# Graph attention on one core: row-by-row fetches shared by two issuing engines and counted on six semaphores

## The chip, the core and the metric

The kernel runs on one core of a Trainium2 chip. The core has a matrix engine (TensorE, "PE"; its weight loads are listed as "PEld"), a vector engine (VectorE, "DVE"), a scalar engine (ScalarE, "ACT"), a programmable engine (GpSimd, "POOL") and an engine without arithmetic that issues transfers (SyncE, "SP"). Each engine works through its own list of instructions in order. Engines wait for each other through semaphores. SP, ACT and POOL can issue DMA transfers, and sixteen DMA engines carry them out. An engine that issues a transfer is occupied while it issues; such instructions are listed as "SPq" or "ACTq".

The metric is the time of one execution on the device in microseconds (us), lower is better. A change is called faster or slower in this text when the time moves by more than 0.2%, which is about what a measurement of this kernel can tell from no change.

## The reference

One layer of graph attention with 12,500 nodes, 128 features, 8 heads of 16 features and 212,500 edges that are sorted by destination:

```python
Q = (x @ WQ).reshape(N, H, dh); K = (x @ WK)...; V = (x @ WV)...
Eh = (edge_attr @ WE).reshape(-1, H, dh)
score = K[src] * Q[dst] / sqrt(dh) * Eh
score = exp(clip(score.sum(-1, keepdims=True), -5.0, 5.0))
wV = segment_sum(V[src] * score, dst); Z = segment_sum(score, dst)
h = x + (wV / (Z + 1e-6)).reshape(N, D)
h = batch_norm(h) * gamma + beta
out = layernorm(x + h)
```

What matters here is `K[src]` and `V[src]`: for every edge one row of 256 float32 numbers (1 KB: K and V side by side) must be fetched from a table in the chip's main memory, at an address that is known only from the data.

## The kernel before

**Tiles and groups.** The edges are cut into 1661 tiles of 128 edges. Four tiles make a window and two windows make a group, so a full group `g` has 8 tiles; there are 208 groups (0 to 207), the last with 5 tiles.

**The table stage.** First the kernel multiplies all nodes with `w_kv` and writes the table `kvd` (K and V of every node) to main memory (`table_rows`, L674). For groups 0 to 7 it does not use the table: it gathers rows of `x` instead (64 gathers by POOL) and projects them itself (`project_main`). Small steps of the edge stage are laid between the steps of the table stage by the list `steps` at L706: among them `place` on the first run of windows, `load_rel` of groups 0, 1 and 2, and `turned_onehot` of groups 0 and 1.

**The gathers.** From group 8 on, each tile of 128 rows is fetched by one indirect DMA that POOL issues (`gather`, L229 and L230). It lands in one of nine buffers called `slot`, each of which holds the 8 tiles of a group. A slot is free again once `message(g)` (L615) has read it; `load_kv` (L284) then queues the gathers of the next pending group. Gathers are issued in the order of groups.

**The row fetches.** Some tiles do not go through POOL. For a group in `by_row` the last of its 8 tiles is fetched row by row: SP issues 128 transfers of 1 KB each (`fetch_rows`, L273). In each group from 8 on, SP first loads 16 node offsets into registers (L275, a `TENSOR_LOAD` on `row_ids`) and then issues 16 row transfers with these offsets (L282). So 128 rows, one tile, take 8 groups, and the tile is used 3 groups after its last row was issued: groups 18, 26, 34, ... 202, which makes 24 tiles (3072 rows). `row_plan` (L58) works out this list. The buffer `byrow` has two copies. Rows use the same eight completion semaphores in turn as all other transfers that SP and ACT issue: each transfer waits until the transfer eight places earlier on these semaphores has landed.

**The main loop (L793 to L845)** records the steps of one group after the other; each engine's order of work follows from it. In the order in which they stand: SP loads edge features four groups ahead (`load`, L495, tile `ea`, three buffers) and the transposed positions (`load_rel`, L406, tile `rb`; for groups 16 and later `load_quad`, L393, four groups at a time in tile `rbq`); then SP issues the rows of this group. DVE multiplies K with Q times E (`products`, L597), PE sums the messages of the previous group (`gather_sum`, L636), DVE reduces and clips the scores (L603, L611), ACT takes the exponential (`clip_exp`, L612 and L613) and does short copies of neighbouring groups, the last of them being `q_mid` (L555); DVE multiplies V with the scores (`message`, L621) and compares destinations (`onehot`, L526). At some groups `place` (L375) transposes the positions of the next 64 windows and writes them to `relT` in main memory; ACT issues these writes.

**The end.** After the last group a normalization over all nodes and a layer norm produce the output (`last_stage`, L920).

Of the kernel before, what the change touches and what calls it, by code (L numbers as in the profile page):

```python
# [21 lines left out]
G = 8  # L22
U = 4
WN = 64
# [5 lines left out]
ROWS = P  # L30
FIRST_ROW = 8
ROW_LAG = 3
ROW_STREAMS = (("SP", 16),)
RQ = 4


LAST = [3, 2]
# [20 lines left out]
def row_plan(sizes):  # L58


    full = sizes.count(U) // 2
    used, plan_ = set(), []
    for _, n in ROW_STREAMS:
        groups, end = [], 0
        while True:
            end += P
            g = FIRST_ROW + -(-end // n) - 1 + ROW_LAG
            while g in used:
                g += 1
            if g >= full:  # L70
                break
            used.add(g)
            groups.append(g)
        plan_.append(groups)
    return plan_


def row_groups(sizes):
    return [2 * g for groups in row_plan(sizes) for g in groups]


@with_exitstack
def gnn_kernel(
# [32 lines left out]
    dram = ctx.enter_context(tc.tile_pool(name="dram", bufs=1, space=bass.MemoryType.DRAM))  # L116
    rows = ctx.enter_context(tc.tile_pool(name="rows", bufs=1))
# [9 lines left out]
    relT = dram.tile([T, P], BF16, name="relT")  # L127

# [32 lines left out]
    rel = rel_i.bitcast(F32)  # L161
# [28 lines left out]
    ident = consts.tile([P, P], F32, name="ident")  # L190
# [58 lines left out]

    by_row, fill = {}, {}  # L250
    row_loads = []
    cols = ids = 0
    for (_, n), groups in zip(ROW_STREAMS, row_plan(usizes)):
        tot = len(groups) * P
        for q in range(-(-tot // n)):
            at = (q % P, cols + q // P * n, min(n, tot - q * n))
            fill.setdefault(FIRST_ROW + q, []).append(at + (groups, q * n))
        for q in range(0, tot // n, P):
            row_loads.append((q, min(P, tot // n - q), cols + q // P * n, n, ids + q * n))
        if tot % n:  # L260
            q = tot // n
            row_loads.append((q, 1, cols + q // P * n, tot % n, ids + q * n))
        cols += -(-tot // (P * n)) * n
        ids += tot
        by_row.update({g: None for g in groups})
# [4 lines left out]
    def parts(g, a, b):  # L270
        return [(a, b - 1), (b - 1, b)] if g in by_row and b == G else [(a, b)]

    def fetch_rows(g):  # L273
        for p, c, n, groups, at in fill.get(g, []):
            _, offs = nc.values_load_multi_w_load_instructions(  # L275
                row_ids[p:p + 1, c:c + n], engines=(ET.SP,), min_val=0, max_val=(N - 1) * 8 * P,
                skip_runtime_bounds_check_because="node ids")
            for r, off in enumerate(offs, at):
                k = groups[r // P]
                if r % P == 0:  # L280
                    by_row[k] = late[0].tile([P, 1, 2 * P], F32, name="byrow", bufs=2)
                nc.sync.dma_start(by_row[k][r % P:r % P + 1, 0, :].bitcast(U8), kvb[ds(off, 8 * P)].unsqueeze(0))  # L282

    def load_kv():  # L284
        while free and pending and table[0]:
# [54 lines left out]
    def within(f, g):  # L340
        return f(g) if 0 <= g < NG else None
# [9 lines left out]
    def vw(a, r):  # L351
        return a[:, ustarts[r[0]]:ustarts[r[0]] + (r[1] - r[0]) * r[2]].rearrange("p (g k) -> p g k", k=r[2])
# [22 lines left out]
    def place(r):  # L375
        nc.vector.tensor_copy(vw(rel, r), vw(rel_i, r))
        nc.vector.tensor_tensor(vw(rel, r), vw(rel, r), bc(base_f, r), op=OP.subtract)
        end = ustarts[r[0]] + (r[1] - r[0]) * r[2]
        for t in range(ustarts[r[0]], end, P):
            n = min(P, end - t)  # L380
            ps = spare_ps
            nc.tensor.transpose(ps[:n], rel[:, t:t + n], ident)
            row = wp.tile([P, P], BF16, name="relrow", bufs=2)
            nc.vector.tensor_copy(row[:n], ps[:n])
            nc.scalar.dma_start(relT[t:t + n, :], row[:n])

    RB = {}

    def load_quad(q):
        t = late[0].tile([P, RQ, U * P], BF16, name="rbq", bufs=2)  # L390
        for h in (0, 1):
            at = ustarts[2 * RQ * q + h] * P
            nc.sync.dma_start(t[h * WN:(h + 1) * WN], bass.AP(  # L393
                tensor=relT.tensor, offset=relT.offset + at, ap=[[0, WN], [G * P, RQ], [1, U * P]]))
        for k in range(RQ):
            RB[RQ * q + k] = t[:, k, :]

    quads = range(-(-2 * FIRST_ROW // RQ), sizes.count(G) // RQ)

    def load_rel(g):  # L400
        if g // RQ in quads:
            return
        RB[g] = wp.tile([P, U * P], BF16, name="rb", bufs=3)
        for h in (0, 1):
            t, n = ustarts[2 * g + h], usizes[2 * g + h]
            nc.sync.dma_start(RB[g][h * WN:(h + 1) * WN, :n * P],  # L406
                              bass.AP(tensor=relT.tensor, offset=relT.offset + t * P, ap=[[0, WN], [1, n * P]]))

    mv = consts.tile([P, 2], F32, name="mv")
    ab = consts.tile([P, 2], F32, name="ab")  # L410
# [180 lines left out]
    def products(g, hs=(0, 1)):  # L591
        if 0 in hs:
            PR[g] = wp.tile([P, G, P], F32, name="p", bufs=1)
        for i in hs:
            a, b = halves(g)[i]
            for c, d in parts(g, a, b):
                nc.vector.tensor_tensor(PR[g][:, c:d, :], KV[g](c, d, 0), PW[g][i][:, c - a:d - a, :], op=OP.mult)  # L597

    def scores(g, h=None):
        a, b = (0, nt(g)) if h is None else halves(g)[h]  # L600
# [14 lines left out]
    def message(g, h=None):  # L615
        if h is not None:
            ranges = parts(g, *halves(g)[h])
        else:
            ranges = halves(g) if g < nxg and g not in SLOT else parts(g, 0, sizes[g])
        for a, b in ranges:  # L620
            nc.vector.tensor_tensor(  # L621
                MSG[g][:, a:b, :P].rearrange("p t (h d) -> p t h d", d=DH),
                KV[g](a, b, P).rearrange("p t (h d) -> p t h d", d=DH),
                exp_ps(g)[:, a:b, :, None].to_broadcast([P, b - a, H, DH]), op=OP.mult)
        if g in SLOT and h != 0:
            free.append(SLOT[g])
            load_kv()
# [546 lines left out]
```

## Time and profile before

| what | value |
|---|---|
| time, median of 3 runs | 2114.01 us (2113.06 to 2116.01) |
| time of the profiled execution | 2108.13 us |
| its span (first to last instruction) | 2106.3 us |
| POOL: gathers from the table | 1573, of 948 ns each |
| SP: row transfers | 3072 |
| PE, DVE, ACT, POOL busy | 80%, 78%, 30%, 75% of the span |
| DMA engines, mean rate | 184 GB/s |

The shares of busy time are means over the whole span. Instructions that issue a DMA from SP or ACT, and loads of registers, are not counted as busy, so a small busy share of ACT does not say how much room its list of instructions has. The chain of waits follows the work that ended last backwards from the last instruction; where an engine waits for nothing that the profile shows, the time is called "issue". A gather by POOL shows as 0.95 us of work and 0.30 us of "issue" behind it.

### The profile page before, as it was taken

What the parts mean: (1) busy time and instruction counts of PE and PEld (TensorE: products, weight loads), DVE (VectorE), ACT (ScalarE), POOL (GpSimd) and SP (SyncE); (2) the same over time, 40 slices, a digit from 0 to 9 for tenths busy, and PEclk for the clock granted to TensorE, in tenths of its full rate; (3) what the DMA queues carried; (4) which work ended last, traced back from release to release, by engine and by line L of the source; (5) the groups of instructions that cost most, each with busy time, mean ns of one, the idle gap of its engine ahead of it and who ended that gap; (6) DMA issues with size and microseconds to landing.
All of it is one profiled execution on the core that took longest, in us unless ns stands there. A gap on an engine that the chain in (4) does not pass through costs nothing.

```text
span 2106.3 us, 37679 instructions
## 1 busy us (share of the span) xinstructions
PE 1692.8 (80%) x9414; PEld 1106.6 (53%) x9414; DVE 1633.1 (78%) x3601; ACT 635.8 (30%) x2480; POOL 1579.5 (75%) x1673
## 2 busy tenths in 40 slices
PE   8899888888777787777778778777777777787777
PEld 6665555555455455445455555554454544454457
DVE  3559989988777778787778787778777778777787
ACT  2353333333222222222222223222222223223225
POOL 7777777777777777777777777777777777777775
PEclk9999989999999999899998898899999999899999
DMA  8956656666566555566565566665566565565684
GB/s 284 306 183 187 188 174 192 188 188 190 166 188 187 175 169 166 159 187 187 177 176 159 165 182 187 178 177 158 168 188 177 177 176 158 166 187 149 181 269 129
DMA packets 177913, 386.83 MB, mean 184 GB/s; under 512 B 38862, under 2 KB 94711, under 8 KB 177687
## 3 DMA queue, kind: packets, MB, share of 16 engines
q0 software_dynamic: 77552, 210.48, 34.1%
q1 hardware_dynamic: 95972, 171.08, 26.7%
q10 hardware_dynamic: 4163, 2.79, 0.4%
q8 instruction: 77, 1.26, 0.2%
q14 instruction: 149, 1.22, 0.2%
HBM read 364.58 MB, written 19.63 MB: 182 GB/s over the span
## 4 chain that ended last, share of the span: by engine, by line
DVE 23%; POOL 22%; DMA 21%; issue 16%; PE 13%; SPq 2%; ACT 2%; DVEq 1%; ACTq 0%; POOLq 0%
POOL slot L230 22%; DMA slot<-kvd,srcs 15%; DVE wt L578 6%; DVE msg L621 4%; DVE s L603 3%; DMA rbq<-relT 3%; PE ps_a L636 3%; PE ps_e L565 2%; DVE p L597 2%; DVE oh L526 2%; DMA ea<-eaT 2%; SPq L282 1%; PE ps_t L586 1%; DVE ot L536 1%; PE ps_m L661 1%
## 5 line engine op out<-in xcount | busy, mean ns | idle before, releaser
L230 POOL DMA_INDIRECT slot<-kvd,srcs x1573 | 1491.0, 948 | 480.5 <-issue 415.2
L636 PE MATMUL ps_a<-msg,oh 128*128 128x136 f32 (+1 forms) x3322 | 555.9, 309 | 0.5 <-DVE msg L621 0.5
L597 DVE TENSOR_TENSOR p<-slot,ps_t 128x512 f32<-128x512 f32 (+1 forms) x410 | 269.2, 672 | 309.8 <-DMA slot<-kvd,srcs 254.2
L636 PEld LDWEIGHTS ps_a<-msg,oh 128*128 128x128 f32 (+1 forms) x3322 | 450.0, 178 | 84.1 <-issue 60.7
L565 PE MATMUL ps_e<-ea,w_e 128*128 128x512 f32 x832 | 438.1, 653 | 32.3 <-DMA ea<-eaT 30.7
L612 ACT ACTIVATE ps_m<-s 128x64 f32<-128x64 f32 (+1 forms) x209 | 47.5, 227 | 1226.0 <-DVE s L611 920.2
L586 PE MATMUL ps_t<-ident,wt 128*128 128x128 f32 x1661 | 249.5, 293 | 113.1 <-DVE wt L578 111.4
L578 DVE TENSOR_TENSOR wt<-wt,ps_q 128x512 f32<-128x512 f32 x416 | 265.6, 680 | 13.0 <-PE ps_q L573 12.5
L661 PE MATMUL ps_m<-ident,at 128*128 128x128 f32 x412 | 99.0, 324 | 218.3 <-DVE oh L529 214.5
L586 PEld LDWEIGHTS ps_t<-ident,wt 128*128 128x128 f32 x1661 | 197.1, 148 | 141.9 <-DVE wt L578 135.3
L567 ACT ACTIVATE wt<-ps_e 128x512 f32<-128x512 f32 x416 | 233.9, 586 | 71.8 <-PE ps_e L565 67.7
L603 DVE TENSOR_REDUCE s<-p 128x64 f32<-128x1024 f32 (+1 forms) x209 | 251.9, 1205 | 0.1
L621 DVE TENSOR_TENSOR msg<-slot,ps_m 128x1024 f32<-128x1024 f32 (+2 forms) x209 | 244.7, 1173 | 1.0 <-ACT ps_m L612 0.7
L565 PEld LDWEIGHTS ps_e<-ea,w_e 128*128 128x128 f32 x832 | 158.3, 212 | 154.4 <-issue 115.8
L661 PEld LDWEIGHTS ps_m<-ident,at 128*128 128x128 f32 x412 | 64.5, 197 | 310.1 <-ACT q L555 283.8
L573 PE MATMUL ps_q<-ot,q 64*128 64x512 bf16 x1248 | 173.1, 384 | 0.0
L573 PEld LDWEIGHTS <-q 64*128 64x128 bf16 x1248 | 44.3, 95 | 195.7 <-issue 171.8
L526 DVE TENSOR_TENSOR oh<-ps_m,rel_i 128x512 f32<-128x512 f32 x208 | 142.0, 683 | 0.0
L515 ACT ACTIVATE xw<-hx 128x64 f32 x416 | 83.9, 248 | 65.2 <-issue 53.0
L652 DVE SCALAR_TENSOR_TENSOR at<-os,keep,rz 128x128 f32<-128x128 f32 x208 | 73.2, 352 | 26.2 <-PE ps_m L661 1.5
L666 ACT ACTIVATE hx<-ps_m 128x64 f32 x412 | 90.4, 219 | 7.9 <-PE ps_m L662 1.2
L546 PE MATMUL ps_m<-w_q,xw 128*128 128x128 f32 x416 | 85.9, 290 | 3.2 <-DVE oh L529 2.8
(173 smaller groups left out, 1549.5 us busy)
## 6 DMA issues: line engine op xcount, KB each, us to landing
ea<-eaT SPq DMA_DIRECT2D x207, 512.0 KB
byrow<-kvd SPq DMA_DIRECT2D x3072, 1.0 KB
slot<-kvd,srcs POOLq DMA_INDIRECT x1573
rbq<-relT SPq DMA_DIRECT2D x94, 256.0 KB
kvd<-slot SPq DMA_DIRECT2D x12, 512.0 KB
kvd<-t SPq DMA_DIRECT2D x12, 512.0 KB
slot<-xT SPq DMA_DIRECT2D x24, 256.0 KB
out<-o SPq DMA_DIRECT2D x23, 256.0 KB
```

The lines of the kernel that those rows point to most:

```text
L230: return nc.gpsimd.indirect_dma_start(out=out, out_offset=None, in_=table, in_offset=bass.IndirectOffsetOnAxis(ap=srcs[:, e:e + 1], axis=0))
L526: nc.vector.tensor_tensor(one, iota_ps[:, None, :].to_broadcast([P, n, P]), r[:, :n, None].to_broadcast([P, n, P]), op=OP.is_equal)
L565: nc.tensor.matmul(eh, w_e, EA[g][:, a:b, :].rearrange("p a b -> p (a b)"), start=True, stop=True)
L567: nc.scalar.activation(t[:, :(b - a) * P], eh, AF.Copy)
L573: nc.tensor.matmul(QE[g][h], Q3[g][r, k, :], OT[g][r, :(b - a) * P], start=(k == 0), stop=(k == 2))
L578: nc.vector.tensor_tensor(t, t, QE[g][h], op=OP.mult)
L586: nc.tensor.transpose(ps[:, j, :], WT[g][h][:, j * P:(j + 1) * P], ident)
L597: nc.vector.tensor_tensor(PR[g][:, c:d, :], KV[g](c, d, 0), PW[g][i][:, c - a:d - a, :], op=OP.mult)
L603: nc.vector.tensor_reduce(SS[g][:, a:b, :], PR[g][:, a:b, :].rearrange("p t (h d) -> p t h d", d=DH), axis=AX.X, op=OP.add)
L621: nc.vector.tensor_tensor(MSG[g][:, a:b, :P].rearrange("p t (h d) -> p t h d", d=DH), KV[g](a, b, P).rearrange("p t (h d) -> p t h d", d=D ...
L636: nc.tensor.matmul(AGG[g][WN if j >= n else 0:], OH[g][j], MSG[g][:, j, :], start=(j == 0), stop=(j == n - 1))
L661: nc.tensor.matmul(ps, AT[g], ident, start=True, stop=False)
```

## The change

Four things are changed together.

1. `fetch_rows` is called twice per group: SP issues 20 rows at its old place in the loop, and ACT issues 12 more rows after its part of `q_mid` and ahead of `message`. Each engine loads its own offsets into registers first. A tile of 128 rows therefore takes 4 groups instead of 8; the tiles are the last ones of groups 14, 18, 22, ... 206, which makes 49 (6272 rows). `byrow` has three copies.
2. The row transfers no longer take part in the eight shared completion semaphores. They add to six semaphores of the kernel's own (`rows_in`), one for each tile in turn. VectorE waits once for each tile, ahead of the product of that tile, until the semaphore has the count of all 128 rows.
3. The transposed positions `relT` are kept in two tensors, one for the first and one for the second window of each group, so that the four groups of `load_quad` lie next to each other and each of 64 partitions is read in one piece of 4 KB instead of four of 1 KB. For this, `place` copies the windows of each kind together before its transposes (VectorE, into a buffer of the name `xt`) and writes two pieces for each transpose instead of one.
4. The tile `rb` has two buffers instead of three.

```diff
-ROW_STREAMS = (("SP", 16),)
+SP_ROWS = 20
+ACT_ROWS = 12
 RQ = 4
+NSEM = 6
...
     full = sizes.count(U) // 2
...
+    groups, end = [], P
+    while FIRST_ROW + -(-end // (SP_ROWS + ACT_ROWS)) - 1 + ROW_LAG < full:
+        groups.append(FIRST_ROW + -(-end // (SP_ROWS + ACT_ROWS)) - 1 + ROW_LAG)
+        end += P
+    return groups
...
+    rows_in = [tc.alloc_semaphore(f"rows_in{i}") for i in range(NSEM)]
...
+    def fetch_rows(g, et, a, b):
...
+        eng = {ET.SP: nc.sync, ET.Activation: nc.scalar}[et]
+        _, offs = nc.values_load_multi_w_load_instructions(
+            row_ids[p:p + 1, c + a:c + b], engines=(et,), min_val=0, max_val=(N - 1) * 8 * P,
+            skip_runtime_bounds_check_because="node ids")
+        for r, off in enumerate(offs, at + a):
+            k = row_tiles[r // P]
+            if r % P == 0:
+                by_row[k] = late[0].tile([P, 1, 2 * P], F32, name="byrow", bufs=3)
+            d = eng.dma_start(by_row[k][r % P:r % P + 1, 0, :].bitcast(U8), kvb[ds(off, 8 * P)].unsqueeze(0))
+            d.then_inc(rows_in[r // P % NSEM], 16)
+            tc.no_tile_sem_insts.add(d.ins.name)
+            tc.add_to_no_dep_group(f"rows{k}", d.ins)
+
+    def rows_there(g):
+        k = row_tiles.index(g)
+        w = nc.vector.wait_ge(rows_in[k % NSEM], 16 * P * (k // NSEM + 1))
+        tc.declare_fence(w.ins, group=f"rows{g}")
...
     def place(r):
...
+        k = r[2]
+        for w in range(r[0], r[1], P // (2 * k) * 2):
+            z = min(w + P // (2 * k) * 2, r[1])
+            stage = wp.tile([P, 4, P], F32, name="xt", bufs=2)[:, 0, :]
+            spans, n = [], 0
+            for v in range(w, min(w + 2, z)):
+                c = len(range(v, z, 2))
+                nc.vector.tensor_copy(stage[:, n:n + c * k].rearrange("p (g k) -> p g k", k=k),
+                                      vw(rel, r)[:, v - r[0]:z - r[0]:2, :])
+                spans.append((v, n, c * k))
+                n += c * k
             ps = spare_ps
-            nc.tensor.transpose(ps[:n], rel[:, t:t + n], ident)
+            nc.tensor.transpose(ps[:n], stage[:, :n], ident)
             row = wp.tile([P, P], BF16, name="relrow", bufs=2)
             nc.vector.tensor_copy(row[:n], ps[:n])
-            nc.scalar.dma_start(relT[t:t + n, :], row[:n])
+            for v, a, m in spans:
+                nc.scalar.dma_start(relT[v % 2][at_half[v]:at_half[v] + m, :], row[a:a + m])
...
-            nc.sync.dma_start(t[h * WN:(h + 1) * WN], bass.AP(
-                tensor=relT.tensor, offset=relT.offset + at, ap=[[0, WN], [G * P, RQ], [1, U * P]]))
+            nc.sync.dma_start(t[h * WN:(h + 1) * WN].rearrange("p k d -> p (k d)"), bass.AP(
+                tensor=relT[h].tensor, offset=relT[h].offset + at_half[2 * RQ * q + h] * P,
+                ap=[[0, WN], [1, RQ * U * P]]))
...
-        RB[g] = wp.tile([P, U * P], BF16, name="rb", bufs=3)
+        RB[g] = wp.tile([P, U * P], BF16, name="rb", bufs=2)
...
             for c, d in parts(g, a, b):
-                nc.vector.tensor_tensor(PR[g][:, c:d, :], KV[g](c, d, 0), PW[g][i][:, c - a:d - a, :], op=OP.mult)
+                if d - c == 1 and g in by_row:
+                    rows_there(g)
+                step = nc.vector.tensor_tensor(PR[g][:, c:d, :], KV[g](c, d, 0), PW[g][i][:, c - a:d - a, :], op=OP.mult)
+                own(g, c, d, step)
...
-        fetch_rows(g)
+        fetch_rows(g, ET.SP, 0, SP_ROWS)
         within(products, g)
...
         within(q_mid, g + 3)
+        fetch_rows(g, ET.Activation, SP_ROWS, SP_ROWS + ACT_ROWS)
         within(message, g)
```

More of the change, by code (lines that the diff above doesn't have):

```diff
@@ L61, in row_plan @@
     full = sizes.count(U) // 2
[L62 to L75, printed above, removed]
+    groups, end = [], P
[3 more added lines that the diff above has]
+    return groups
 def row_groups(sizes):
-    return [2 * g for groups in row_plan(sizes) for g in groups]
+    return [2 * g for g in row_plan(sizes)]
 @with_exitstack
@@ L126, in gnn_kernel @@
     kvd = dram.tile([N, 2 * P], F32, name="kvd")
-    relT = dram.tile([T, P], BF16, name="relT")
+    at_half, half_rows = [], [0, 0]
+    for w, k in enumerate(usizes):
+        at_half.append(half_rows[w % 2])
+        half_rows[w % 2] += k
+    relT = [dram.tile([n, P], BF16, name=f"relT{h}") for h, n in enumerate(half_rows)]
     small_ps = psp.tile([P, 4, P], F32, name="ps_m", bufs=1)
@@ L251, in gnn_kernel @@
     row_loads = []
[L252 to L265, printed above, removed]
+    n = SP_ROWS + ACT_ROWS
+    row_tiles = row_plan(usizes)
+    tot = len(row_tiles) * P
+    for q in range(-(-tot // n)):
+        fill[FIRST_ROW + q] = (q % P, q // P * n, q * n)
+    for q in range(0, tot // n, P):
+        row_loads.append((q, min(P, tot // n - q), q // P * n, n, q * n))
+    if tot % n:
+        q = tot // n
+        row_loads.append((q, 1, q // P * n, tot % n, q * n))
+    cols = -(-tot // (P * n)) * n
+    by_row.update({g: None for g in row_tiles})
+    rows_in = [tc.alloc_semaphore(f"rows_in{i}") for i in range(NSEM)]
     row_ids = consts.tile([P, cols], I32, name="row_ids")
@@ L271, in parts, with own @@
         return [(a, b - 1), (b - 1, b)] if g in by_row and b == G else [(a, b)]
[L273 to L282, printed above, removed]
+    def fetch_rows(g, et, a, b):
+        if g not in fill:
+            return
+        p, c, at = fill[g]
+        b = min(b, tot - at)
+        if b <= a:
+            return
+        eng = {ET.SP: nc.sync, ET.Activation: nc.scalar}[et]
[14 more added lines that the diff above has]
+        tc.declare_fence(w.ins, group=f"rows{g}")
+    def own(g, a, b, step):
+        if g in by_row and b == G and b - a == 1:
+            tc.declare_no_dep(step.ins, group=f"rows{g}", reason="the semaphore of the rows")
     def load_kv():
@@ L402, in load_rel @@
             return
-        RB[g] = wp.tile([P, U * P], BF16, name="rb", bufs=3)
+        RB[g] = wp.tile([P, U * P], BF16, name="rb", bufs=2)
         for h in (0, 1):
-            t, n = ustarts[2 * g + h], usizes[2 * g + h]
-            nc.sync.dma_start(RB[g][h * WN:(h + 1) * WN, :n * P],
-                              bass.AP(tensor=relT.tensor, offset=relT.offset + t * P, ap=[[0, WN], [1, n * P]]))
+            n = usizes[2 * g + h]
+            nc.sync.dma_start(RB[g][h * WN:(h + 1) * WN, :n * P], bass.AP(
+                tensor=relT[h].tensor, offset=relT[h].offset + at_half[2 * g + h] * P, ap=[[0, WN], [1, n * P]]))
     mv = consts.tile([P, 2], F32, name="mv")
@@ L620, in message @@
         for a, b in ranges:
-            nc.vector.tensor_tensor(
+            step = nc.vector.tensor_tensor(
                 MSG[g][:, a:b, :P].rearrange("p t (h d) -> p t h d", d=DH),
@@ L624, in message @@
                 exp_ps(g)[:, a:b, :, None].to_broadcast([P, b - a, H, DH]), op=OP.mult)
+            own(g, a, b, step)
         if g in SLOT and h != 0:
```

4 lines of the change are left out of this document (removed).

## The prediction

> **What bounds the kernel now.** I read the page's busy shares and slices first, then POOL's timeline where its row could break, then the issue lists of SP and ACT, because the change works there, and last the vector engine's list near the end.
>
> ```profile
> PE 1692.8 (80%) x9414; PEld 1106.6 (53%) x9414; DVE 1633.1 (78%) x3601; ACT 635.8 (30%) x2480; POOL 1579.5 (75%) x1673
> ...
> POOL 7777777777777777777777777777777777777775
> ...
> L230 POOL DMA_INDIRECT slot<-kvd,srcs x1573 | 1491.0, 948 | 480.5 <-issue 415.2
> ```
>
> PE and DVE look busier than POOL, but POOL's sevens have no gap: each gather is 0.95 us of work plus 0.30 us of "issue" that always follows. POOL's timeline at three places (start, duration, idle time before and its releaser):
>
> ```profile
> 82.01 0.94 POOL L230 DMA_INDIRECT slot<-x,srcs  x1 [0.30 <-DVE qr L554]
> 83.78 0.94 POOL L230 DMA_INDIRECT slot<-kvd,srcs  x1 [0.82 <-DMA rb<-relT]
> ...
> 172.89 1.04 POOL L230 DMA_INDIRECT slot<-kvd,srcs  x1 [0.30 <-issue]
> 174.71 0.94 POOL L230 DMA_INDIRECT slot<-kvd,srcs  x1 [0.78 <-DVE msg L621]
> ...
> 2053.53 0.95 POOL L230 DMA_INDIRECT slot<-kvd,srcs  x1 [0.31 <-issue]
> 2063.90 0.20 POOL L925 MEMSET pick<- 128x128 bf16 x1 [9.43 <-PE ps_m L662]
> ```
>
> The table's gathers run from 83.78 to 2054.48 us: 1970.7 us for 1573, or 1.253 us each. The one wait for a free slot that shows is 0.48 us, at 174.71. So POOL is the bound, from 84 us on: the span is 83.8 us before it, 1573 times 1.253, and 51.9 us after it. The chain of waits gives POOL 22% only, since it walks through whichever engine released the last wait. I follow POOL's list instead.
>
> The other engines have room. Between 299.98 and 307.49 us two exponentials follow each other without a wait for a gather: 7.51 us for a group, while POOL needs 8 times 1.253 = 10.0 us. Compute catches up with POOL near 510 us, and from there DVE waits for gathers (247.5 us in 96 waits between 520 and 2020 us).
>
> **Part 1: fewer gathers.** 49 row tiles stand in place of 24, so 25 gathers go: 25 x 1.253 = -31.3 us, all of it on the path as long as POOL's list stays unbroken. Of this, the tile of group 14 is worth nothing: group 17's first gather already waits for the slot that the message of group 8 frees, and would arrive 1.25 us earlier and wait 1.25 us longer (bounds 0 and 1.25; I take 1.25, as that wait is there).
>
> **Part 2: what the rows cost SP.** (Of a tile: count, then min/median/max ns of one; of the timeline: start, duration.)
>
> ```profile
> L275 SPq TENSOR_LOAD <-row_ids x192: 1150/1196/1488, 168.3 to 1991.9; - x192
> ...
> 1208.47 0.37 SPq L495 DMA_DIRECT2D ea<-eaT  x1
> 1210.18 5.31 SPq L282 DMA_DIRECT2D byrow<-kvd  x16
> 1215.59 0.36 SPq L495 DMA_DIRECT2D ea<-eaT  x1
> ...
> L510 ACTq TENSOR_LOAD <-base_i x208: 482/492/1746, 36.6 to 2027.8; - x104
> ```
>
> An unblocked group on SP takes 1215.59 - 1208.47 = 7.12 us with 16 rows, 0.33 us a row. A register load takes 492 ns for 2 values and 1196 ns for 16, 0.05 us a value. Twenty rows: 7.12 + 4 x 0.33 + 4 x 0.05 = 8.64 us, and the two issues of `load_quad` (607 ns each, every fourth group) add 0.30: 8.9 us. Queued behind the rows on SP is the next `ea` load, and PE waits for that. POOL's new pace is (3 x 8 + 7) x 1.253 / 4 = 9.71 us a group, but SP starts its rows at 168 us, 84 us behind POOL, and must have issued group 203's by about 1995 us: 195 groups at (1995 - 168) / 195 = 9.37 us. With 8.9 SP is at 95% of that. So SP sets the pace of the early groups (8.9 for 7.5 us), compute, some 80 us behind POOL at group 8 and gaining 9.71 - 8.9 = 0.8 a group, meets it after about 100 groups, near 1050 us instead of 510, and SP then has room. Cost zero; the cover is 0.47 us a group.
>
> SP also loses something: a row now waits for no earlier transfer. SP's waits at the row line were 140.0 us behind writes of `relT` and 100.6 us behind `rbq`. These go and SP runs ahead until it waits for a free `ea` buffer (206.7 us before). That waiting is not on POOL's path, so I count nothing.
>
> **Part 3: what they cost ACT.** A register load of 12 values (0.49 + 10 x 0.05 = 1.0 us) and 12 issues; no row of one partition was issued by ACT, so I take SP's 0.33 us (bounds: 0.26, the 228 ns of the instruction and one 29 ns move, and 0.42, ACT's 327 ns for `relT` plus the same gaps; SP's rows are nearest in shape). Sum 5.0 us (4.1 to 6.0). Behind them is the exponential of the next group (timeline, then the list of waits: total, times, longest):
>
> ```profile
> 302.84 0.30 ACT L555 ACTIVATE q<-qr 128x128 bf16<-128x128 f32 x1
> 307.49 0.23 ACT L612 ACTIVATE ps_m<-s 128x64 f32<-128x64 f32 x1 [4.36 <-DVE s L611]
> ...
> ACT ps_m L612 <- DVE s L611: 920.2, 161, 10.0
> ```
>
> ACT is free for 4.4 us in a tight group and 920.2 / 161 = 5.7 us on the mean. A tight group gets 0.6 us longer (0 to 1.6), 8.1 us, still under 9.37. No cost, except at the end (below).
>
> **Part 4: VectorE.** 25 more products and messages are split. Seven tiles and one cost 0.56 + 0.28 for 0.69 us and 1.08 + 0.28 for 1.21 us: +0.3 us a tile, 7.5 us in all, under DVE's waits for gathers. The one wait per tile replaces waits on eight semaphores. Rows are issued at least two groups ahead of use, and DVE waited for rows 8.2 us in 3 waits before; behind a late row stand the products, and PE behind those. Zero, by the same cover.
>
> **Part 5: `place`, `relT`, `rb`.** In the loop, four more short copies and two more issues at six places lie under the waits for gathers. In the table stage they are ahead of POOL's first table gather, which already came 0.52 us late. Four copies (bounded by 0 and 4 x 0.29, from the 128x128 casts of that step) and two ACT issues of 0.33 us: 0 to 1.8 us. With two `rb` buffers the load for group 2 must wait for `turned_onehot(0)`: it was issued at 59.68 us and that step ended at 64.92, so SP stands 5 us there, with table writes and a load of `hx` behind it; SP itself was idle from 63.9 to 65.9 and caught up. Bounds 0 and 3 us in all, I take 0.8, nearer to zero because the table writes end at 79 us. Longer pieces of `rbq` take DMA time away; nobody on the path waits for them.
>
> **Part 6: the end.**
>
> ```profile
> 2023.51 0.69 DVE L597 TENSOR_TENSOR p<-slot,ps_t 128x512 f32<-128x512 f32 x1 [2.00 <-DMA slot<-kvd,srcs]
> ...
> 2057.24 0.42 DVE L597 TENSOR_TENSOR p<-slot,ps_t 128x256 f32<-128x256 f32 x1 [0.17 <-DMA slot<-kvd,srcs]
> ```
>
> After 2023.51 DVE works without a wait for a gather until the last one, 0.17 us: compute and POOL arrive together. Group 206 now has a row tile, so POOL's last four groups take 1.25 us less while compute takes 0.3 us more and ACT up to 0.6 more. Bounds 0 and 2.2; I take 1.2.
>
> **Sum:** -31.3 + 1.25 + 0.8 + 1.2 = -28.0 us. Against the profiled execution: 2108.1 - 28.0 = 2080.1. The median of the runs shown lies 5.9 us higher, so I predict 2114.0 - 28.0 = 2086.0.
>
> **Rivals.** *The two issuing queues hold each other up (slower).* SP's rows and ACT's rows are now issued at the same time. If one must wait while the other issues, each of ACT's 12 issues costs SP up to 0.228 us: 8.9 + 2.7 = 11.6 us a group, and the span 168 + 195 x 11.6 + 83 = 2513 us (83 from group 203's product to the end). It is slower than before once SP's group passes (2106 - 251) / 195 = 9.51 us, 0.05 us for each of ACT's issues. Before, both queues issued together only seldom:
>
> ```profile
> 109.20 0.34 SPq L495 DMA_DIRECT2D ea<-eaT  x1
> ...
> 109.21 0.35 ACTq L177 DMA_DIRECT2D rel_i<-dst  x1
> ```
>
> Neither is longer than alone (363 and 327 ns are the medians), which speaks against it. A fifth of the full price, 0.05 us an issue, could hide in such rows: 9.5 us a group, span 2104, no change. The Trainium skill has such a rule (Perfetto Trace Analysis, section DMA Instruction — HWDGE (DVE, Sync)): the block that makes descriptors is shared by the two issuing sequencers and locked for one at a time, and the wait for the lock is inside the profiled duration. By that rule the forecast would be the slower one above; the pair at 109.20 does not agree with it.
>
> *SP falls behind at the end (smaller gain).* Rows now run to group 203 (before: 199), beside the final loads of `x` (four issues per freed slot, 0.46 us apart in the chain at 1999.78 us): 10.8 us a group for five groups, 5.5 us late. The `ea` loads lead by 2.5 groups, some 24 us, less a landing of 7.1 (the chain at 2001.25 us). Only if SP is already 12 us behind does it cost; then up to 10 us: 2096.
>
> *The transfers are counted, but compute was the bound anyway (no change).* That would need POOL to wait for slots; it waited 0.5 us once. 2114.
>
> **Chances.** Forecast 0.75, own range 2080 to 2091 (no correction at all and 1.5 us of scatter; all at their upper bounds); late end 0.10; no change 0.03; queues holding each other up 0.12. I leave out most of the last: range 2080 to 2102. Faster 0.85, same 0.03, slower 0.12.
>
> **What would show it.** POOL's list unbroken, 1548 gathers of 1.25 us, from about 84.6 to about 2025 us; 1.8 us of idle ahead of group 17's gather; SP rows 0.33 us apart also where ACT issues; ACT rows some 0.33 us apart; DVE's waits for gathers smaller and starting later. I am wrong if SP's rows lengthen beside ACT's, if PE waits long for `ea` after 1200 us, or if POOL shows gaps.

## The result and the profile after

| what | before | after |
|---|---|---|
| time, median of 4 runs each | 2113.53 us (2112.16 to 2116.01) | 2092.09 us (2090.14 to 2094.42) |
| ratio | | 0.9898, 95% interval 0.9881 to 0.9915 |
| time of the profiled execution | 2108.13 us | 2092.52 us |
| its span | 2106.3 us | 2090.7 us |

The change makes the kernel faster by 21.4 us, 1.0%. The forecast was 28.0 us: 2086.0, in a range from 2080 to 2102. The sign and the bound came out as forecast and the time lies in the range; the missing 6.6 us are the subject of what follows.

The page of the changed kernel: busy times, POOL's slices, and its group of gathers (count, busy time and mean ns, then idle time before them).

```profile
PE 1676.2 (80%) x9414; PEld 1095.7 (52%) x9414; DVE 1643.1 (79%) x3679; ACT 631.2 (30%) x2480; POOL 1561.5 (75%) x1648
...
POOL 7677777777777777777777777777777777777775
...
L227 POOL DMA_INDIRECT slot<-kvd,srcs x1548 | 1472.3, 951 | 479.3 <-issue 410.6
```

There are 25 gathers fewer, and POOL's sevens again have no gap. ACT's busy share is 30% as before, although ACT now issues 2352 rows: those instructions are not in this share. That will matter below.

POOL's timeline at the same three places as before the change (start, duration, idle time before and its releaser):

```profile
82.72 0.95 POOL L227 DMA_INDIRECT slot<-x,srcs  x1 [0.30 <-issue]
88.09 1.05 POOL L227 DMA_INDIRECT slot<-kvd,srcs  x1 [4.43 <-DMA ea<-eaT]
...
176.31 0.95 POOL L227 DMA_INDIRECT slot<-kvd,srcs  x1 [0.30 <-issue]
180.03 0.95 POOL L227 DMA_INDIRECT slot<-kvd,srcs  x1 [2.77 <-DVE msg L647]
...
2034.35 0.95 POOL L227 DMA_INDIRECT slot<-kvd,srcs  x1 [0.30 <-issue]
```

The first table gather starts at 88.09 us, 4.3 us later than before; the wait for the slot at group 17 has grown from 0.48 to about 2.5 us (the idle time less the 0.30 that every gather has); the last gather ends at 2035.30 us instead of 2054.48. From there to the end are 55.4 us instead of 51.9.

The rows and their register loads (count, then min/median/max ns of one, first and last start; two answers, by the tiles `byrow` and `row_ids`):

```profile
L284 SPq DMA_DIRECT2D byrow<-kvd x3920: 224/228/586, 181.2 to 2021.7; - x196
L284 ACTq DMA_DIRECT2D byrow<-kvd x2352: 222/223/687, 180.5 to 2014.5; - x196
```

```profile
L277 SPq TENSOR_LOAD <-row_ids x196: 1372/1442/1764, 179.5 to 2014.0; - x196
L277 ACTq TENSOR_LOAD <-row_ids x196: 768/810/992, 179.5 to 2009.5; - x196
```

A row occupies ACT for 223 ns and SP for 228 ns. Sorted by whether a row of ACT was being issued at the same time, SP's rows take 232.5 ns on the mean beside one (1784 rows) and 230.3 ns without (2136 rows).

What VectorE waited for at its products, first before and then after the change, and what SP waited for after it (total us, times, longest us; answers of the list of waits):

```profile
DVE p L597 <- DMA slot<-kvd,srcs: 254.2, 100, 6.6
```

```profile
DVE p L622 <- DMA slot<-kvd,srcs: 192.0, 96, 5.1
...
DVE p L622 <- DVEq L291: 71.3, 18, 5.2
```

```profile
SPq L518 <- PE ps_e L588: 100.1, 54, 5.5
SPq L429 <- DVE ot L559: 44.4, 9, 6.1
```

L291 is the new wait of VectorE for a row tile. It took 71.3 us, all of it before 860 us. SP's waits at its row line for `relT` and `rbq` (140.0 and 100.6 us before) are gone. What is left on SP are waits for a free `ea` buffer (L518) and, new, for a free `rb` buffer (L429).

### The profile page after: what moved, and what is told of

Its sections match the earlier page's. It is cut to its first block, busy times and chain, and to the rows that moved or that the text cites. A ratio compares the mean times of both kernels' runs of the same rounds, so it can differ in the third digit from the quotient of the medians.

```text
span 2090.7 us, 44264 instructions
## 1 busy us (share of the span) xinstructions
PE 1676.2 (80%) x9414; PEld 1095.7 (52%) x9414; DVE 1643.1 (79%) x3679; ACT 631.2 (30%) x2480; POOL 1561.5 (75%) x1648
## 5 line engine op out<-in xcount | busy, mean ns | idle before, releaser
L227 POOL DMA_INDIRECT slot<-kvd,srcs x1548 | 1472.3, 951 | 479.3 <-issue 410.6
L663 PE MATMUL ps_a<-msg,oh 128*128 128x136 f32 (+1 forms) x3322 | 547.6, 306 | 0.9 <-DVE msg L647 0.9
L663 PEld LDWEIGHTS ps_a<-msg,oh 128*128 128x128 f32 (+1 forms) x3322 | 443.3, 176 | 83.7 <-issue 59.2
L588 PE MATMUL ps_e<-ea,w_e 128*128 128x512 f32 x832 | 432.9, 646 | 23.2 <-DMA ea<-eaT 20.6
L622 DVE TENSOR_TENSOR p<-slot,ps_t 128x512 f32<-128x512 f32 (+1 forms) x410 | 263.7, 663 | 210.9 <-DMA slot<-kvd,srcs 192.0
L638 ACT ACTIVATE ps_m<-s 128x64 f32<-128x64 f32 (+1 forms) x209 | 47.5, 227 | 1200.5 <-DVE s L637 845.0
L590 ACT ACTIVATE wt<-ps_e 128x512 f32<-128x512 f32 x416 | 229.1, 585 | 44.2 <-PE ps_e L588 43.0
```

Source lines behind the costliest of these rows:

```text
L227: return nc.gpsimd.indirect_dma_start(out=out, out_offset=None, in_=table, in_offset=bass.IndirectOffsetOnAxis(ap=srcs[:, e:e + 1], axis=0))
L588: nc.tensor.matmul(eh, w_e, EA[g][:, a:b, :].rearrange("p a b -> p (a b)"), start=True, stop=True)
L590: nc.scalar.activation(t[:, :(b - a) * P], eh, AF.Copy)
L622: step = nc.vector.tensor_tensor(PR[g][:, c:d, :], KV[g](c, d, 0), PW[g][i][:, c - a:d - a, :], op=OP.mult)
L663: nc.tensor.matmul(AGG[g][WN if j >= n else 0:], OH[g][j], MSG[g][:, j, :], start=(j == 0), stop=(j == n - 1))
```

## The experiments

**The same two kernels once more, together on one chip.** No edit; the kernel before once, the changed one in four executions.

> The kernel before once more, on the chip of the next three. In the two profiles so far the median distance between two gathers is 1251 ns before and 1254 ns after, which over 1548 gathers is 4.6 us. Theory A (it belongs to the chip or the execution): the distance here equals that of the changed kernel on this same chip within 1 ns. Theory B (the row transfers slow POOL): here some 3 ns less than with the change. The table's gathers start at 83.8 us, and the first one of group 17 waits some 0.5 us.

> The changed kernel again, beside the kernel before. Theory A: 21 us faster (18 to 25), the first table gather at 88 us, the same distance between gathers as before on this chip. Theory B: distance 3 ns above that of before.

The changed kernel took 2087.96 us (2083.10 to 2089.55), the kernel before 2109.4 us (median of 7), a ratio of 0.9900 (0.9883 to 0.9916): again 21.4 us. The traces of this pair show where the gain went:

| us from the start | before | after | difference |
|---|---|---|---|
| first table gather starts | 83.24 | 86.14 | +2.9 |
| last gather of group 205 ends | 2039.0 | 2011.6 | -27.4 |
| last product of group 205 starts | 2041.0 | 2014.98 | -26.0 |
| last gather of all ends | 2055.26 | 2026.72 | -28.5 |
| span | 2106.7 | 2081.3 | -25.4 |

Half of the gathers lie 1.251 us or less apart in both of these traces. In the first trace of the changed kernel that median was 1.254, and it was 3 ns above the one of before already between 3 and 84 us, where no row is issued. So the rows do not slow POOL; this is a difference between executions (1548 x 3 ns = 4.6 us). The traced execution of the changed kernel was the shortest of its four, which is why the traces differ by 25.4 us and the medians by 21.4. These 4 us I leave to the scatter; the traces of the first pair differ by 15.6 us, and its medians by 21.4 too.

The products near the end, first of the kernel before, then of the changed one of this second pair (VectorE's timeline):

```profile
2024.30 0.69 DVE L597 TENSOR_TENSOR p<-slot,ps_t 128x512 f32<-128x512 f32 x1 [1.90 <-DMA slot<-kvd,srcs]
2032.36 1.28 DVE L597 TENSOR_TENSOR p<-slot,ps_t 128x512 f32<-128x512 f32 x2
2040.36 1.27 DVE L597 TENSOR_TENSOR p<-slot,ps_t 128x512 f32<-128x512 f32 x2
```

```profile
2014.98 0.69 DVE L622 TENSOR_TENSOR p<-slot,ps_t 128x512 f32<-128x512 f32 x1 [1.89 <-DMA slot<-kvd,srcs]
2023.79 0.68 DVE L622 TENSOR_TENSOR p<-slot,ps_t 128x512 f32<-128x512 f32 x1
2025.18 0.55 DVE L622 TENSOR_TENSOR p<-slot,ps_t 128x384 f32<-128x384 f32 x1
2025.64 0.28 DVE L622 TENSOR_TENSOR p<-byrow,ps_t 128x128 f32<-128x128 f32 x1
```

Before, the last wait for a gather is in group 203 (2024.30) and 204 and 205 follow without one. After, the last wait is in group 205 (2014.98), and the products of group 206 and its row tile (2025.64) wait for nothing. From the last product of group 205 to the end both need the same: 65.7 and 66.3 us. So what counts of POOL's list is its part up to group 205, with 24 gathers fewer, not 25.

**Three `rb` buffers, two of `byrow`.** The changed kernel with two numbers exchanged.

```diff
-                by_row[k] = late[0].tile([P, 1, 2 * P], F32, name="byrow", bufs=3)
+                by_row[k] = late[0].tile([P, 1, 2 * P], F32, name="byrow", bufs=2)
...
-        RB[g] = wp.tile([P, U * P], BF16, name="rb", bufs=2)
+        RB[g] = wp.tile([P, U * P], BF16, name="rb", bufs=3)
```

> The change with three buffers of rb and two of byrow. The first table gather came 4.3 us later with the change. Theory A (the load of rb for group 2 waits for a buffer and holds up the loads of hx behind it on SP): first table gather at 84 to 85 us, the wait of group 17's first gather unchanged, 3 to 4 us faster than the change as it is. Theory B (the longer place holds up the table stage): no difference, first table gather at 88 us.

SP's timeline in the table stage (start, duration), first of the changed kernel in the first pair, then with three buffers:

```profile
59.17 0.37 SPq L716 DMA_DIRECT2D kvd<-slot  x1
65.25 1.09 SPq L429 DMA_DIRECT2D rb<-relT  x2
66.43 0.54 SPq L716 DMA_DIRECT2D kvd<-slot  x1
67.02 0.50 SPq L518 DMA_DIRECT2D ea<-eaT  x1
67.57 0.94 SPq L152 DMA_DIRECT2D hx<-xT  x1
```

```profile
59.23 0.37 SPq L716 DMA_DIRECT2D kvd<-slot  x1
59.66 2.05 SPq L429 DMA_DIRECT2D rb<-relT  x2
61.81 0.52 SPq L716 DMA_DIRECT2D kvd<-slot  x1
62.38 0.57 SPq L518 DMA_DIRECT2D ea<-eaT  x1
62.99 1.14 SPq L152 DMA_DIRECT2D hx<-xT  x1
```

With two buffers SP stands 5.7 us ahead of the load for group 2, and the load of `hx` behind it goes out 4.6 us later (67.57 for 62.99). PE then waits 3.2 us for `hx` (2.8 in the second pair), and not at all with three. With three, the first table gather starts at 83.60, as before the change. So the `rb` buffer is the whole price of the start. The kernel took 2085.19 us (2084.22 to 2089.45), ratio 0.9890 (0.9874 to 0.9907); the interval overlaps that of the changed kernel. In its trace POOL's last gather ends 2.1 us earlier (2024.58), but the end from there is 58.1 us instead of 54.6: the last product of group 205 starts 5.4 us after its last gather was issued, not 3.4, and compute from there takes 67.7 us. The start that was won did not reach the end in this execution.

**The rows alone.** As the last one, and also `relT`, `place` and the loads of `rb` and `rbq` as in the kernel before.

```diff
-    relT = [dram.tile([n, P], BF16, name=f"relT{h}") for h, n in enumerate(half_rows)]
+    relT = dram.tile([T, P], BF16, name="relT")
...
-            for v, a, m in spans:
-                nc.scalar.dma_start(relT[v % 2][at_half[v]:at_half[v] + m, :], row[a:a + m])
+            nc.scalar.dma_start(relT[t:t + n, :], row[:n])
```

> The change in its rows alone: relT, place and the loads from it as before, three buffers of rb, two of byrow. Theory A: the start as with three buffers of rb within 1 us, and the same time within 2 us, since relT is not on POOL's path. Theory B (place delays the table stage): first table gather at 84 us, 4 us faster than the change as it is, and faster than three buffers of rb alone by the same. If the longer pieces of rbq matter to the landing of the gathers, this one is some us slower at its end.

2084.39 us (2081.83 to 2085.06), ratio 0.9878 (0.9862 to 0.9895); first table gather at 84.50, last gather ends at 2024.83, span 2082.0. The two halves of `relT` and the longer pieces of `rbq` are worth nothing that these runs can tell; all of the gain is in the rows. This is the fastest version that was measured, but its interval touches that of the changed kernel, so it is not shown to be faster.

**The six semaphores alone.** The rows alone with the numbers of before: 24 tiles. This and the next three experiments ran on another chip than the second pair; the kernel before took 2108.98 us there.

```diff
-SP_ROWS = 20
-ACT_ROWS = 12
+SP_ROWS = 16
+ACT_ROWS = 0
```

> The kernel before with one part of the change alone: the rows' own six semaphores with one wait of VectorE per tile. 16 rows a group on the sync engine, none on ScalarE, 24 tiles, relT and its loads as before. Theory (GpSimd's list sets the end, the semaphores only free the sync engine): 1573 gathers at 1.251 us, span 2105 to 2108 us, ratio 1.000 within 0.002; the sync engine's waits at its row line for relT and rbq (140.0 and 100.6 us before) are gone and its waits for a free ea buffer grow by about as much. Rival (waiting on rows through shared semaphores delayed the path): the span falls by 5 us or more with the same number of gathers. Rival (the extra wait of VectorE costs): slower by 24 times 0.05 to 0.3 us, 1 to 7 us.

2109.92 us (median of 10) against 2108.98 (17), ratio 1.000 (0.999 to 1.001). The traced execution was the slowest of the ten, with gathers 1.254 us apart where 1.251 was expected. SP's waits (first here, then in the kernel before of the second pair):

```profile
SPq L505 <- PE ps_e L575: 467.5, 163, 11.3
```

```profile
SPq L495 <- PE ps_e L565: 209.8, 70, 11.2
SPq L282 <- DMA relT<-relrow: 140.1, 9, 26.9
SPq L282 <- DMA rbq<-relT: 96.8, 94, 2.0
```

The 236.9 us at the row line are gone, and the wait for a free `ea` buffer has grown by 257.7 us. Freed time on an engine that has room turns into another wait.

**The rows on the shared semaphores.** The changed kernel, 20 and 12 rows, without its own six.

```diff
-            d.then_inc(rows_in[r // P % NSEM], 16)
-            tc.no_tile_sem_insts.add(d.ins.name)
-            tc.add_to_no_dep_group(f"rows{k}", d.ins)
...
-                if d - c == 1 and g in by_row:
-                    rows_there(g)
```

> The changed kernel without its own semaphores: 20 rows on the sync engine and 12 on ScalarE count on the shared ones of the transfers, and VectorE has no wait of its own for them. Theory (the own semaphores let rows be issued back to back): rows wait for earlier transfers on their semaphore; before, 1.2 us of such waits a group lay on the sync engine (240.6 us in 195 groups) and it had 1.7 us of room; with 20 rows 8.9 + 1.5 = 10.4 us a group against 9.4 to be had, so the sync engine sets the pace: 168 + 195 x 10.1 to 10.4 + 83 = 2220 to 2280 us; ScalarE's rows show waits too. Rival (there is room enough without them): 2085 to 2092 us, as the changed kernel.

2646.1 us (2640.9 to 2655.4), 25.6% slower than before. From its two lists of waits, of all engines and of SP, with the lines of the changed kernel (first pair) between them:

```profile
ACT ps_m L632 <- DMA byrow<-kvd: 901.6, 145, 8.7
...
PE ps_e L584 <- DMA ea<-eaT: 510.7, 140, 10.0
...
DVE qr L573 <- ACT hx L687: 379.3, 171, 5.8
DVE p L616 <- DMA byrow<-kvd: 312.8, 46, 7.9
```

```profile
ACT ps_m L638 <- DVE s L637: 845.0, 145, 9.4
...
DVE qr L577 <- ACT hx L693: 30.7, 17, 5.0
...
PE ps_e L588 <- DMA ea<-eaT: 20.6, 13, 2.9
```

```profile
SPq L284 <- DMA byrow<-kvd: 388.0, 528, 5.4
SPq L411 <- DMA byrow<-kvd: 177.6, 55, 6.2
```

Rows now wait for earlier rows to land. SP's pitch in a group (from one row to the next, on the mean) rises from 332 to 443 ns, ACT's from 347 to 508 ns. I had put a price on SP's side only, 2220 to 2280 us, and too small a one: SP waits 388.0 us at its rows and 177.6 us at the loads of `rbq` behind them, 2.9 us a group where I took 1.5. Its period is 12.3 us a group, and PE waits 510.7 us for `ea`, which SP issues behind its rows. On ACT the exponentials stand behind waiting rows, and VectorE waits for ACT's next copy 379.3 us instead of 30.7. The 901.6 us are no measure of this: ACT's idle time before the exponential is 845.0 us in the changed kernel too, where it is released by VectorE. Which of the two engines costs more is not separated by a run. So the six semaphores are worth nothing with 16 rows on SP and over 500 us with 32 rows on two engines (2646.1 us for the 2088 of the changed kernel): they are what makes the other part possible.

**All 32 rows on SP.** The version with three `rb` buffers.

```diff
-SP_ROWS = 20
-ACT_ROWS = 12
+SP_ROWS = 32
+ACT_ROWS = 0
```

> The changed kernel with three rb buffers and two of byrow, and all 32 rows of a group issued by the sync engine, none by ScalarE; 49 tiles as in the change. Theory (what limits rows is the issuing engine's 0.33 us a row and 0.05 us a register value): 8.9 + 12 x 0.38 = 13.5 us a group, span 168 + 195 x 13.0 to 13.5 + 83 = 2786 to 2884 us, POOL's list full of gaps that wait for slots. Rival (rows are limited by something that the two queues share, landing or descriptor making, so that where they are issued is of no account): 2080 to 2092 us.

2908.28 us in one execution, span 2906.4. SP's timeline in the middle (start, duration of the run of rows, count):

```profile
1208.81 10.65 SPq L284 DMA_DIRECT2D byrow<-kvd  x32
1219.56 0.37 SPq L518 DMA_DIRECT2D ea<-eaT  x1
```

32 rows in 10.65 us are 0.333 us each. SP's period is 13.67 us a group on the mean (median 13.42), and 168 + 195 x 13.67 + 83 = 2917. The limit is the issuing engine: the same rows over two engines take 8.9 us a group. The period lies 0.17 us above my upper figure of 13.5, which is why the time lies just above my range.

**16 rows on ACT.** The version with three `rb` buffers, 20 and 16 rows: 55 tiles, six gathers fewer.

```diff
-ACT_ROWS = 12
+ACT_ROWS = 16
```

> The changed kernel with three rb buffers and two of byrow, and 16 rows a group by ScalarE in place of 12: 55 tiles in place of 49, six gathers fewer. Theory (GpSimd's list is still the bound, ScalarE has 5.7 us of waits a group for its 12 or 16 rows): -6 x 1.251 = -7.5 us against the kernel with 12 rows and the same buffers (span 2082.6), less 1 to 2 us at the end where compute is last: span 2075 to 2078. ScalarE's rows take 6.0 us a group. Rival (ScalarE's row issue is on the path at every group: 1.3 us more of it): 2085 us and more, and VectorE's waits for gathers fall to under 100 us.

2102.13 us (2097.78 to 2106.28), ratio 0.9970 (0.9959 to 0.9981): most of the gain is lost again, and the span of 2097.5 us lies far above the 2075 to 2078 of my theory. Waits, ACT's timeline (the four writes of `relT` stand in this group only), and SP's rows (min/median/max ns):

```profile
DVE p L622 <- DMA slot<-kvd,srcs: 34.5, 18, 3.2
```

```profile
1203.66 5.18 ACTq L284 DMA_DIRECT2D byrow<-kvd  x16
1208.93 2.48 ACTq L408 DMA_DIRECT2D relT<-relrow  x4
1211.52 0.23 ACT L638 ACTIVATE ps_m<-s 128x64 f32<-128x64 f32 x1 [8.40 <-DMA relT<-relrow]
```

```profile
L284 SPq DMA_DIRECT2D byrow<-kvd x3920: 224/228/1755, 169.9 to 2032.9; - x196
```

Between 1000 and 1900 us ACT is occupied for 8.8 us of a group of 9.55 (arithmetic and issuing together, gaps under 0.15 us counted in), against 7.1 of 9.72 with 12 rows and 3.1 of 9.85 before. VectorE hardly waits for gathers now, and POOL's list has gaps: its distances over 1.3 us add up to 26.8 us more than 1.251 each, against 5.0 with 12 rows. Of these, 11.0 us stand ahead of a group's first gather, where POOL waits for a slot. POOL's list alone is no longer the bound. That ACT has no room for 16 rows is the likely reason: VectorE waits 202.8 us for the copies behind ACT's exponential, 25.1 with 12 rows. It is not the only suspect. With 16 rows, 62 of SP's rows took 0.6 to 1.8 us, 59 of them while ACT was issuing a row; with 12 rows and the same buffers none took so long. PE's waits for `ea` rose from 16.6 to 63.9 us. No run separates the two.

**Four runs on a slow chip.** These were to settle the end and the room on ACT: a version without the tile of group 206, one with most loads of `x` behind the loop (twice), and one with 14 rows on ACT, all made from the rows alone.

```diff
-    row_tiles = row_plan(usizes)
+    row_tiles = row_plan(usizes)[:-1]
```

```diff
-        while free and todo and not pending:
+        while free and len(todo) > NY - 8 and not pending:
             load_x()
```

```diff
-ACT_ROWS = 12
+ACT_ROWS = 14
```

> The rows alone as above, but without the 49th row tile, that of group 206: one gather more at the end of GpSimd's list. Theory (after group 205 compute is the last, so this tile saves nothing): the last gather ends 1.25 us later, from there to the end is 1.25 us less, the span stays (2082.0 within the scatter of 3 us), and VectorE does not wait for a gather of group 206. Rival (GpSimd's list sets the end to the last, as the prediction counted for all tiles but one): +1.25 us, and a wait of VectorE for the gathers of group 206.

> The rows alone (relT, place and the loads of rb and rbq as before, three rb buffers, two of byrow; 20 and 12 rows), and of the 25 loads of x into freed slots only the first 8 inside the loop, the other 17 behind it, once GpSimd has only group 206 and 207 left. Theory (these loads, between 1975 and 2012 us, are what makes the last gathers of groups 203 to 205 land 5.2, 5.3 and 6.1 us after their issue ends, measured as the start of the waiting product): with them gone it is 2.0 to 3.7 us, as in the steady part, and since compute alone follows group 205, the span falls by 2 to 3 us against 2082.0; from the last gather to the end 54 to 55 us in place of 57.2. Rival (the rows themselves delay the gathers): 5 to 6 us stays and so does the span. Rival (the loads come too late for the final sums): waits of GpSimd or VectorE for slot<-xT after 2041 us and a span of 2085 or more.

> The rows alone as above, with 14 rows a group by ScalarE in place of 12: 52 tiles, three gathers fewer. Theory (ScalarE is occupied 7.2 us of a group with 12 rows, of it 3.4 computing, and 8.8 with 16, where a group of compute came out at 9.4 to 9.6 us and GpSimd waited 26.7 us in all for slots; GpSimd needs 9.7): with 14 rows 8.0 us occupied and 9.2 us a group, still under GpSimd's 9.68: POOL's list has no gaps over 2 us, -3 x 1.251 = -3.75 us against 2082.0, less about 1 at the end: span 2079 to 2080.5; VectorE waits for gathers 60 to 150 us. Rival (every row of ScalarE is on the path): between 12 rows and 16 (2082.6 and 2097.5), 2088 to 2092, POOL with 5 to 15 us of gaps.

> The kernel of c3_latex again, on another chip, because on the one where that batch ran every engine's instructions came in bursts (the kernel before took 2750 us there), which hides the question. Theory (the loads of x between 1975 and 2012 us make the last gathers of groups 203 to 205 land late): the waiting products of 203 to 205 start 2.0 to 3.7 us after their gathers end in place of 5.2, 5.3 and 6.1; from the last gather to the end 54 to 55 us in place of 57.2; span 2079 to 2080 where the execution has gathers 1.251 us apart. Rival (the rows themselves delay the gathers): 5 to 6 us stays, 57 us stays. Rival (the loads come too late for the final sums): waits for slot<-xT after 2041 us and a span of 2085 or more.

On this chip the kernel before took 2750 us (9 executions, 2746 to 2761), and the versions 3100.3, 3101.3 and 3120.5 us, 12.5 to 13.4% slower than it. The repeat came to the same chip and gave 3097.4 us, 12.9% slower. None of the expectations can be judged by this, since POOL is not the bound there: in the repeat its distances over 1.3 us add up to 923 us more than 1.251 each. From the trace of the repeat, waits and SP's timeline:

```profile
PE ps_e L575 <- DMA ea<-eaT: 554.2, 102, 13.2
```

```profile
1200.29 0.86 SPq L505 DMA_DIRECT2D ea<-eaT  x1
1201.17 0.02 SPq L403 DMA_DIRECT2D rbq<-relT  x2
1202.70 6.68 SPq L280 DMA_DIRECT2D byrow<-kvd  x20
1209.42 0.33 SPq L505 DMA_DIRECT2D ea<-eaT  x1
```

A run of 20 rows without a disturbance takes 6.68 us, as elsewhere. But 31% of SP's rows start over 0.6 us after the one before (2% with the rows alone on the earlier chip): in stretches SP's instructions come about 0.7 us apart, even its moves between registers. SP's period is 14.25 us a group instead of 9.39, and its rows run from 247.8 to 3033.2 us, nearly the whole span. PE waits 554.2 us for `ea`, which SP issues behind its rows. So there SP seems to set the pace, and more rows on it cost time; the kernel before was not traced there. Gathers are 1.251 us apart there too. What makes SP's instructions come in bursts on that chip is open. The changed kernel itself did not run there.

## Why the prediction was right, and where it was off

**What is missing.** Of the 6.6 us, the terms of Parts 5 and 6 below make up 4.1 in the second pair of traces and 5.9 in the first. The rest is within the scatter of single executions.

**The bound and the main term hold.** POOL's list stayed unbroken, and each gather taken from it gave 1.251 us. Of the 25 that were counted (-31.3), 24 lie ahead of the point that decides (-30.0).

**Part 1, the slot wait.** Taken as +1.25. The distance ahead of group 17's first gather grew by 0.6 us in the second pair (2.46 to 3.07) and by 1.9 in the first (1.82 to 3.72). The mechanism was right; its size is not exact to a microsecond, and the 1.9 lies outside the bounds of 0 and 1.25.

**Part 2, SP.** Forecast 8.9 us a group with 0.33 us a row; the changed kernel's trace of the second pair has a median period of 8.87 and 332 ns a row. Compute met POOL near 890 us (first long wait for a gather; 822 in the first trace) instead of 1050; that changes nothing.

**Part 3, ACT.** Forecast 0.33 us a row, bounds 0.26 to 0.42; measured 347 ns on the mean inside a group. The cover was real, and with 16 rows it is used up.

**Part 4, VectorE.** It was taken to wait for rows as little as before (8.2 us in 3 waits); it waited 71.3 us in 18 waits. It cost nothing all the same, for the reason given in Part 2: all of them lie before 860 us, where SP sets the pace and compute is behind POOL.

**Part 5, the start.** This term was mis-sized: 0.8 with bounds of 0 and 3; measured 2.9 in the second pair and 4.3 in the first. The step that failed is "SP itself was idle from 63.9 to 65.9 and caught up". SP did catch up with its table writes, but the load of `hx` behind the wait went out 4.6 us later, and PE waited 3.2 us for it. The run with three buffers shows that this wait is the cause. The idle time of an engine does not pay for a delay of what is issued ahead of it.

**Part 6, the end.** Also mis-sized: 1.2 with bounds of 0 and 2.2; measured 3.2 in the second pair (51.4 to 54.6) and 3.6 in the first. By the table above it consists, in the second pair, of three parts: the tile of group 206 saves nothing, since compute alone follows group 205 (1.25); the last product of group 205 starts 3.4 us after its last gather instead of 1.9 (1.5); and compute takes 0.6 us more. The first is what the 1.2 stood for, the third lay within the bounds, and the second was not counted at all. Why these gathers land later was to be shown by the runs on the slow chip and stays open. That the final loads of `x` now start earlier and lie beside them is only argued: in the kernel before, the late products are those of groups 202 and 203, which lie beside these loads there.

**The sum** for the second pair: -30.0 + 2.9 - 0.3 = -27.4 to the end of group 205's gathers, + 1.5 + 0.6 = -25.3, against a span shorter by 25.4. The -0.3 is what is left over, with the +0.6 of the slot wait in it. For the first pair: -30.0 + 4.3 + 1.9 for the slot wait + 4.6 for the 3 ns of each gather + 1.2 left over = -18.0, + 1.8 + 0.5 = -15.7, against 15.6.

**The rivals.** In the changed kernel the two queues do not hold each other up: 232.5 for 230.3 ns a row, and none of SP's rows takes over 0.6 us. The rule of the Trainium skill (Perfetto Trace Analysis, section DMA Instruction — HWDGE (DVE, Sync)), a wait for the shared block inside the profiled duration, does not show between SP and ACT in it. With 16 rows on ACT some of SP's rows do lengthen beside ACT's, 253.2 for 234.3 ns on the mean and up to 1.755 us; why is open, so this rival is refuted for the change and not for more rows. Where SP's period rose far above 9.51 us a group, the price that this rival was given, the kernel was slower than before by hundreds of microseconds: 12.3 us with shared semaphores, 13.7 with 32 rows, 14.3 on the slow chip. SP was not late at the end: after 1200 us the list of waits shows none of PE for `ea`, in either trace of the changed kernel. That compute was the bound anyway is refuted by 24 gathers that gave their full price.

## What to carry to other kernels

Where one engine's unbroken list is the bound, each instruction taken from it gives its full distance, up to the point where another engine has the last word; find that point at the end before counting. Moving issues to a second engine uses time that its busy share does not show: add arithmetic and issuing per stage (here 7.1 of 9.7 us was good, 8.8 of 9.55 was not). A buffer taken away is not free because the waiting engine has idle time; ask what is issued behind the wait and who needs it.

## What was not expected of the hardware

- The distance between POOL's gathers is 1.251 us in some executions and 1.254 in others, on the same chip (1.254 without the tile of group 206 and 1.251 with the late loads, both on the slow chip) and for the same kernel (1.254 and 1.251 for the changed one). Over 1548 gathers that is 4.6 us, about the scatter between executions.
- On one of the chips SP's instructions come in bursts about 0.7 us apart, and the kernel before takes 2750 us for 2109. Its gathers, the time of a row without a disturbance (228 ns) and VectorE's reductions (1.21 us) are as elsewhere.
- A one-row transfer occupies ACT for 223 ns at the median and SP for 228, but on the mean ACT's take longer (250 for 231 ns): the first of each twelve takes 0.47 us on the mean, where on SP the first of twenty takes 0.27 us.
- With 16 rows a group on ACT, 62 of SP's 3920 rows took 0.6 to 1.755 us, 59 of them while ACT was issuing. In the changed kernel, and with 12 rows and the same buffers, none took over 0.6 us.
